# Joint column instructions in a 3x3 convolution: two row combinations in one tile, both output columns read by one instruction

## The chip, the cores and the metric

The kernel runs on one core of one Trainium2 chip. The core has a matrix engine (TensorE, PE in the profile; its weight loads are a row of their own, PEld), a vector engine (VectorE, DVE), a scalar engine (ScalarE, ACT), GpSimd (POOL) and SyncE (SP), each with its own queue of instructions; DMA queues are filled from SP, ACT and POOL. [...] The metric is the device time of one launch in microseconds, the median of the runs of the kernel. All data are float32.

## The reference

Two residual bottleneck blocks, one after the other, on 64 images of 1024 channels and 14x14 points. Each block is

```
out = relu(bn(conv1x1(x,   w1)  + b1))     # 1024 -> 256
out = relu(bn(conv3x3(out, w2)  + b2))     # 256 -> 256, padding 1
out = bn(conv1x1(out, w3) + b3)            # 256 -> 1024
out = relu(x + softplus(residual_scale) * out)
```

with `bn` the normalization by mean and variance over all images and points. The change lies in the 3x3 convolution (`conv2`), which runs once a block.

## The kernel before, in words

**The whole.** A first stage computes the 1x1 convolution of block 0 (0 to 307 us). Then, for each block, come `conv2`, the statistics of the third convolution, and the third convolution with the residual sum, which for block 0 is fused with the first convolution of block 1. `conv2` lies at about 307 to 602 us and 1292 to 1586 us. The activations of one block, `y_all`, stay in SBUF: 128 partitions, 2 channel slots, 8 groups (`NG`) of 8 images (`GI`). Within a group the rows come first: a row (`LINE`) is 8 images x 14 columns = 112 elements, and the columns of an image are stored as seven odd ones and then seven even ones, so a half row is one column of a pair.

**The arithmetic of `conv2` (L540).** It is a fast 3x3 convolution. Along the rows, a tile of four output rows is made from six row combinations of the input, one for each of `NF` = 6 transformed filters (`us`, made in the first stage and kept in DRAM). They are used in pairs: filters 1 and 2, 3 and 4, 5 and 0 (`order`, L542). Filters 3 and 4 need three tiles of rows (`full`), the others four (`RT`). Within a row combination `r`, every pair of columns is made from three inputs, by `Input.make` (L601): `sums` (the sum of both columns), `diffs` (their difference) and `v` (steps between neighbours of the same parity, whose two edge columns are copied by ACT, L612 and L613). `sums` and `diffs` have 448 elements a partition (336 for three tiles), `v` 768 (576), without its edges.

**The matmuls.** `Products` (L678) holds one filter of one group. Its four kinds of matmul are `m` (on `sums`), `l` (on `diffs`), `even` and `odd` (on `v`), each as two output slots times two input slots; the profile counts eight records for each. ACT copies `m` out of its bank into the banks `even` and `odd` (L710 with the bias, L712), PE adds the `v` products there, ACT copies `l` into SBUF as `ls` (L719), and DVE forms the output columns: even + ls and odd - ls (`add`, L744, recorded at L753). The banks are `l`, `m`, `odd` and `even`, two of each.

**The order of PE.** All matmuls are kept in program order (`matmul`, L167). The loop at L908 runs over 48 filters: `l` of this filter, `even`, then `m` of the next filter with ACT's copies, a long piece of ACT work (`long_work`, L888: the normalization of the next group, or moments of the group before), then `odd`. After that the outputs of this filter go to `finish` (L765), and one more filter's inputs are made, three filters ahead (L906 and L923). PE, in its own order, waits at an `m` until its `sums` are there, and at an `l` until its `diffs` are.

**DVE.** What it does in a group is: the row combinations (`combine`, L576: for filters 1 and 2 four scaled sums `t`, L646 and L647, and `ra`, `rb`; for 3 and 4 two differences and two scaled sums; for 5 and 0 two further differences, L668 and L673, and two scaled sums), six times `make`, six times the two output columns, and the sums that put the output rows together in `finish` (`fa`, `fb`, `fc`, and the four rows of `y`). In the first six groups (`by_transfer`, L772) the last filter's outputs go to `y` and the sum `a` of the earlier ones is added by two accumulating DMAs on POOL (L836). Except where `keep_in_program_order` is called, the order of DVE and ACT is planned when the kernel is built, from the order of the program and from what is ready; it is then fixed. Buffers are counted per name in `BUFS` (L70); a name that isn't in it has one.

## Time and profile before

Median of three runs: 1988.76 us (1988.5 to 1989.09).

| What | Profiled execution |
|---|---|
| span, first to last instruction | 1985.8 us |
| PE matmul | 1925.8 us, 97% |
| PE weight load | 1619.0 us, 82% |
| DVE | 1603.6 us, 81% |
| ACT | 976.0 us, 49% |
| POOL | 541.0 us, 27% |
| granted PE clock, mean | 0.990 |
| chain that ended last | PE 88%, DVE 6%, DMA 3%, ACT 1%, issue 1% |

The median lies 3.0 us above the span of the profiled execution. In the profile's lines the first fields are start and duration in us, the engine, the line of the kernel (helpers have one line for all their calls: every matmul is at L169, every scaled sum at L572), the operation, and output<-inputs by tile names. A number in square brackets is how long the engine had been idle, with what released it. Busy shares are means over stages with different limits, so a stage must be looked at by itself.

### The profile page before, as it was taken

The numbers are of one execution on the slowest core, as the hardware profiler recorded it, in microseconds if no ns is written. First come the engines' busy times: TensorE is split into PE (matmuls) and PEld (weight loads), VectorE is DVE, ScalarE is ACT, GpSimd is POOL, SyncE is SP. The second block draws the span as 40 slices with busy tenths as digits, with TensorE's granted clock in tenths as the row PEclk, the third lists the DMA queues.
The fourth block names the chain that finished last, engine by engine and source line by source line (L and its number), as shares of the span: only waits on it lengthen the run. The fifth ranks groups of instructions, "written<-read, shape, count | busy, mean of one in ns | idle before, by whom it ended". The sixth has DMA issues, their size and how long they took to land.

```text
span 1985.8 us, 27403 instructions
## 1 busy us (share of the span) xinstructions
PE 1925.8 (97%) x9432; PEld 1619.0 (82%) x9432; DVE 1603.6 (81%) x2890; ACT 976.0 (49%) x2007; POOL 541.0 (27%) x638
## 2 busy tenths in 40 slices
PE   8999998999998999999999999989999899999998
PEld 5555557999997889999999999989999887555554
DVE  5778758999998566776777777699999975899997
ACT  1222214566665055555555555446666641555555
POOL 0111100100105134334333433201010050666665
PEclk9999999999998999999999999999999999999999
DMA  7776724676747534444444444257666375699998
GB/s 288 272 257 240 255 98 155 183 206 185 204 143 201 194 130 163 177 182 162 181 177 163 184 173 163 98 181 204 198 186 206 122 196 207 247 335 337 340 340 296
DMA packets 188985, 408.41 MB, mean 206 GB/s; under 512 B 24944, under 2 KB 165136, under 8 KB 172336
## 3 DMA queue, kind: packets, MB, share of 16 engines
q1 hardware_dynamic: 161728, 324.66, 47.6%
q0 software_dynamic: 21504, 30.94, 6.7%
q10 hardware_dynamic: 5616, 51.06, 6.1%
q8 instruction: 75, 1.23, 0.2%
q14 instruction: 62, 0.51, 0.1%
HBM read 263.75 MB, written 115.34 MB: 191 GB/s over the span
## 4 chain that ended last, share of the span: by engine, by line
PE 88%; DVE 6%; DMA 3%; issue 1%; ACT 1%; SPq 0%; POOL 0%; DVEq 0%; ACTq 0%; POOLq 0%
PE ay L169 17%; PE cy L169 14%; PE cp L169 11%; PE ap L169 10%; PE even L169 7%; PE m L169 7%; PE odd L169 7%; PE l L169 7%; PE ax L169 5%; PE cx L169 4%; DVE x L447 2%; DMA x<-mid 1%; PE ps L169 1%; DVE x L505 1%; DMA out<-x 1%
## 5 line engine op out<-in xcount | busy, mean ns | idle before, releaser
L321 ACT ACTIVATE cu<-cy,scale 128x196 f32<-128x196 f32 (+1 forms) x552 | 257.0, 474 | 295.1 <-PE cy L169 287.4
L321 ACT ACTIVATE x<-x,shift 128x392 f32<-128x392 f32 x368 | 212.0, 614 | 69.8 <-POOL x L473 53.2
L447 DVE SCALAR_TENSOR_TENSOR x<-cp,scale,x 128x196 f32<-128x196 f32 (+1 forms) x368 | 177.9, 483 | 82.0 <-PE cp L169 81.0
L169 PE MATMUL cy<-ct,ws 128*128 128x196 f32 (+1 forms) x736 | 221.7, 383 | 2.5 <-ACT cu L321 2.5
L468 POOL TENSOR_TENSOR x<-x,cu 128x196 f32<-128x196 f32 (+1 forms) x184 | 167.7, 911 | 170.5 <-ACT cu L321 170.4
L169 PE MATMUL ay<-at,ws 128*128 128x196 f32 (+1 forms) x752 | 209.3, 381 | 1.0 <-ACT au L321 1.0
L473 POOL TENSOR_TENSOR x<-x,cu 128x392 f32<-128x392 f32 x124 | 126.1, 1017 | 190.8 <-DVE x L447 186.1
L169 PEld LDWEIGHTS ay<-at,ws 128*128 128x128 f32 x752 | 136.3, 190 | 35.1 <-ACT au L321 1.9
L169 PEld LDWEIGHTS cy<-ct,ws 128*128 128x128 f32 x736 | 133.5, 190 | 37.0 <-ACT cu L321 4.1
L169 PE MATMUL m<-sums,ua 128*128 128x224 f32 (+1 forms) x752 | 146.5, 338 | 15.9 <-issue 15.9
L169 PE MATMUL even<-v,ub 128*128 128x224 f32 (+1 forms) x768 | 151.3, 338 | 0.0
L169 PE MATMUL odd<-v,ub 128*128 128x224 f32 (+1 forms) x768 | 151.0, 337 | 0.0
L169 PE MATMUL l<-diffs,ub 128*128 128x224 f32 (+1 forms) x768 | 148.8, 336 | 0.0
L494 POOL TENSOR_TENSOR x<-x,cu 128x392 f32<-128x392 f32 x120 | 125.2, 1044 | 82.2 <-DVE x L447 73.3
L169 PEld LDWEIGHTS m<-sums,ua 128*128 128x128 f32 x752 | 130.5, 189 | 20.7 <-issue 20.4
L836 POOL DMA_DIRECT2D y<-fa x24 | 31.1, 1530 | 414.5 <-ACT ls L719 225.6
L169 PEld LDWEIGHTS even<-v,ub 128*128 128x128 f32 x768 | 135.4, 189 | 1.5
L169 PEld LDWEIGHTS odd<-v,ub 128*128 128x128 f32 x768 | 134.9, 188 | 1.3
L169 PEld LDWEIGHTS l<-diffs,ub 128*128 128x128 f32 x768 | 134.6, 189 | 0.5
L321 ACT ACTIVATE au<-ay 128x196 f32<-128x196 f32 (+1 forms) x141 | 53.6, 380 | 156.9 <-PE ay L169 156.3
L447 DVE SCALAR_TENSOR_TENSOR x<-cx,scale,x 128x196 f32<-128x196 f32 (+1 forms) x184 | 89.1, 484 | 49.9 <-PE cx L169 49.6
L169 PE MATMUL cy<-y,w 128*128 128x196 f32 (+1 forms) x404 | 126.4, 399 | 0.0
(216 smaller groups left out, 4256.7 us busy)
## 6 DMA issues: line engine op xcount, KB each, us to landing
x<-in_x SPq DMA_DIRECT2D x62, 1568.0 KB, 6.6
ub<-u SPq DMA_DIRECT2D x94, 768.0 KB, 4.9
x<-mid SPq DMA_DIRECT2D x32, 1568.0 KB, 9.9
mid<-x ACTq DMA_DIRECT2D x31, 1568.0 KB, 5.1
out<-x SPq DMA_DIRECT2D x123, 392.0 KB, 7.0
ua<-u SPq DMA_DIRECT2D x94, 256.0 KB, 3.0
u<-y POOLq DMA_DIRECT2D x48, 256.0 KB, 6.0
home<-y SPq DMA_DIRECT2D x90, 96.0 KB, 3.8
```

Source lines behind the costliest of these rows:

```text
L169: tc.keep_in_program_order(nc.tensor.matmul(*args, **kw))
L321: tc.keep_in_program_order(nc.scalar.activation(*args, **kw))
L447: nc.vector.scalar_tensor_tensor(v, bank, self.scale[:, o : o + 1], v, ALU.mult, ALU.add)
L468: nc.gpsimd.tensor_add(self.part(1, 1), self.part(1, 1), u3)
L473: nc.gpsimd.tensor_add(v, v, self.u12)
L494: nc.gpsimd.tensor_add(v, v, self.u12[:, i * self.n : (i + 1) * self.n])
L505: nc.vector.tensor_scalar(v, v, self.shift[:, o : o + 1], 0.0, ALU.add, ALU.max)
L836: nc.gpsimd.dma_start(out=out_rows[0][:, o], in_=a[:, o], accum_op=ALU.add)
```

## The change

The two filters of a pair get one tile each for `r`, `v`, `sums` and `diffs` (class `Inputs`), and `sums`, `v` and `diffs` are made by one instruction for both (`add_columns`, `step_columns`, `subtract_columns`). The sums of both are issued before the first filter of the pair is handed on, the steps and differences after it, that is one turn of the loop later; only the first pair of the first group still does it by filter and by slot. The four `t` become two (two neighbouring rows at once), the row differences of filters 3, 4, 5 and 0 are one instruction over twelve rows of both slots (tile `steps`), and filter 0's input takes its rows out of it by ACT copies. `even` and `odd` become one tile of two banks (`columns`), two buffers; ACT copies `l` twice, as +l and -l, and one DVE instruction forms both output columns. In the first six groups the first output row is now written from `a` and `c` (with its last line by an ACT copy), and the accumulating DMA adds the last filter's outputs, from `f`. Buffers: `v`, `sums` and `diffs` two (of pairs), `r`, `steps` and `fa` one, `f` three; before, `r` and `t` had four, `fa` two.

```diff
@@ -67,7 +67,7 @@
 GPX = GI * HW
 RT, NF = 4, 6
 LINE = GI * W
-BUFS = dict(ua=3, ub=3, t=4, r=4, sums=3, diffs=4, v=3, ls=3, f=2, fa=2)
+BUFS = dict(ua=3, ub=3, sums=2, diffs=2, v=2, ls=3, f=3)
 PARTS = 4
@@ -544,9 +543,14 @@
         each = list(itertools.product(range(MS), range(MS)))
-        for tag in COLUMNS * 2:
+        def columns():
+            return psum.pool.tile([P, 2, 512], FP, tag="columns", name="columns", bufs=2)
+        for banks in (columns(), columns()):
             n = MS * RT * GI * WH
-            matmul(psum.tile(n, tag), ident, ident[:, :1].to_broadcast([P, n]), start=True, stop=True)
+            for q in (ODD, EVEN):
+                matmul(banks[:, q, :n], ident, ident[:, :1].to_broadcast([P, n]), start=True, stop=True)
         full = RT - 1
@@ -566,59 +570,60 @@
         def last(to, g, k, by, s=slice(0, MS)):
...
+            nc.scalar.activation(to[:, s], y_grp[:, s, g, 4 * (RT - 1) + k - 1, :], AF.Copy, scale=by)
         def stt(to, a, by, c):
             return nc.vector.scalar_tensor_tensor(to, a, by, c, ALU.mult, ALU.add)
...
+        both = slice(0, MS)
+        steps = []
+        def scratch():
+            return pool.tile([P, MS * 4 * full * LINE], FP, tag="steps", name="steps")
+        class Inputs:
+            def __init__(self, pair, run):
+                self.pair, self.run = pair, run
+                self.tiles = tiles = full if pair[0] == 3 else RT
+                self.lines = lines = tiles * GI
+                n = len(pair) * MS * lines
+                def part(tag, width):
+                    v = pool.tile([P, 2 * MS * RT * GI * width], FP, tag=tag, name=tag, bufs=BUFS.get(tag, 1))
+                    return v[:, : n * width].rearrange("p (k s l c) -> p k s l c", k=2, s=MS, c=width)
+                self.r, self.v = part("r", W), part("v", W)
+                self.sums, self.diffs = part("sums", WH), part("diffs", WH)
+            def rows(self, k):
+                return self.r[:, k].rearrange("p s (r i) w -> p s r (i w)", i=GI)
+            def add_columns(self, k=slice(0, 2), s=both):
+                r = self.r[:, k, s]
+                self.run(nc.vector.tensor_add(self.sums[:, k, s], r[:, :, :, :, WH:], r[:, :, :, :, :WH]))
+            def step_columns(self, k=slice(0, 2), s=both):
+                r, v = self.r[:, k, s], self.v[:, k, s]
+                q = r.rearrange("p k s l (q c) -> p (k s l) q c", q=2)
+                self.run(
+                    nc.vector.tensor_sub(
+                        v[:, :, :, :, 1 : W - 1].rearrange("p k s l (q c) -> p (k s l) q c", q=2),
+                        q[:, :, :, 1:], q[:, :, :, : WH - 1],
                     )
...
+                )
+                nc.scalar.activation(v[:, :, :, :, 0], r[:, :, :, :, 0], AF.Copy)
+                nc.scalar.activation(v[:, :, :, :, W - 1], r[:, :, :, :, W - 1], AF.Copy, scale=-1.0)
+            def subtract_columns(self, k=slice(0, 2), s=both):
+                r = self.r[:, k, s]
+                self.run(nc.vector.tensor_sub(self.diffs[:, k, s], r[:, :, :, :, :WH], r[:, :, :, :, WH:]))
+            def products(self, g, k):
+                i = self.pair[k]
                 first = g == 0 and i == order[0][0]
                 u = {}
@@ -631,49 +636,72 @@
                             in_=us[b][i][:, part, :, a:e].rearrange("p s o k m -> p (s o) (k m)"),
                         )
                     u[a] = v
...
+                return Products(i, self.lines, self.v[:, k], self.sums[:, k], self.diffs[:, k], u, first)
+        def combine(g, pair, before=None):
+            def run(ins):
+                if before is not None:
+                    tc.keep_in_program_order(ins)
+            x = Inputs(pair, run)
+            ra, rb = (x.rows(k) for k in range(2))
             if pair[0] == 1:
...
+                t = scratch()[:, : MS * RT * 2 * LINE].rearrange("p (s r l) -> p s r l", s=MS, r=RT)
+                t2, t1 = t[:, :, :, :LINE], t[:, :, :, LINE:]
                 slots = [both] if before is None else [slice(s, s + 1) for s in reversed(range(MS))]
                 for part in slots:
                     if before is not None:
                         before(part.start)
...
+                    last(t1[:, :, RT - 1], g, 2, -3.0, part)
+                    last(t2[:, :, RT - 1], g, 1, -3.0, part)
                     for s in range(part.start, part.stop):
...
+                        two_rows = y_all[:, s, g * GPX : g * GPX + 4 * full * LINE]
+                        two_rows = two_rows.rearrange("p (r h l) -> p r h l", r=full, h=2)
+                        run(stt(t[:, s, :full], two_rows[:, :, 0], -4.0, two_rows[:, :, 1]))
                     run(nc.vector.tensor_add(ra[:, part], t1[:, part], t2[:, part]))
...
+                    if before is not None:
+                        for make in x.add_columns, x.step_columns, x.subtract_columns:
+                            make(slice(0, 1), part)
                 nc.vector.tensor_sub(rb, t1, t2)
...
+                if before is None:
+                    x.add_columns()
+                else:
+                    for make in x.add_columns, x.step_columns, x.subtract_columns:
+                        make(slice(1, 2))
             elif pair[0] == 3:
...
+                d = scratch().rearrange("p (s f) -> p s f", s=MS)
+                y = y_all[:, :, g * GPX : (g + 1) * GPX]
+                ins = nc.vector.tensor_sub(d, y[:, :, 2 * LINE :], y[:, :, : (H - 2) * LINE])
+                if g == 0:
+                    tc.keep_in_program_order(ins)
+                steps[:] = [d.rearrange("p s (r k l) -> p s r k l", k=4, l=LINE)]
+                d = steps[0]
+                stt(ra, d[:, :, :, 0], 2.0, d[:, :, :, 1])
+                stt(rb, d[:, :, :, 0], -2.0, d[:, :, :, 1])
+                x.add_columns()
             else:
...
+                d = steps[0]
+                last(ra[:, :, RT - 1], g, 1, -1.0)
+                r5, r0 = (r[:, :, :full] for r in (ra, rb))
+                stt(r5, d[:, :, :, 0], -4.0, d[:, :, :, 2])
+                nc.scalar.activation(rb[:, :, 0], y_grp[:, :, g, 1], AF.Copy, scale=-1.0)
+                nc.scalar.activation(rb[:, :, 1:full], d[:, :, : full - 1, 3], AF.Copy, scale=-1.0)
+                nc.scalar.activation(rb[:, :, RT - 1], d[:, :, full - 1, 3], AF.Copy, scale=-4.0)
+                stt(r0, r0, 4.0, d[:, :, :, 1])
+                x.add_columns()
+            yield x.products(g, 0)
+            if before is None:
+                x.step_columns()
+                x.subtract_columns()
+            yield x.products(g, 1)
         class Products:
@@ -701,10 +729,11 @@
             def start(self):
                 self.ls = None
-                self.banks = {q: self.bank(COLUMNS[q]) for q in (EVEN, ODD)}
+                self.banks = columns()[:, :, : MS * self.n].rearrange("p q (o n) -> p q o n", o=MS)
                 if not self.first:
                     m = self.whole("m", SUM, self.sums)
-                    for v in self.banks.values():
+                    for q in (EVEN, ODD):
+                        v = self.banks[:, q]
                         if self.i == 1:
                             for o in range(MS):
                                 nc.scalar.activation(v[:, o], m[:, o], AF.Identity, bias=par[:, B2 + o : B2 + o + 1])
@@ -714,9 +743,10 @@
             def middle(self):
                 l = self.whole("l", DIFF, self.diffs)
-                ls = pool.tile([P, MS * RT * GI * WH], FP, tag="ls", name="ls", bufs=BUFS["ls"])
-                self.ls = ls[:, : MS * self.n].rearrange("p (o n) -> p o n", o=MS)
-                nc.scalar.activation(self.ls, l, AF.Copy)
+                ls = pool.tile([P, 2 * MS * RT * GI * WH], FP, tag="ls", name="ls", bufs=BUFS["ls"])
+                self.ls = ls[:, : 2 * MS * self.n].rearrange("p (q o n) -> p q o n", q=2, o=MS)
+                for q, sign in (EVEN, 1.0), (ODD, -1.0):
+                    nc.scalar.activation(self.ls[:, q], l, AF.Copy, scale=sign)
             def columns(self, *qs):
                 parts = {ODD: [(D3M1, self.r[:, :, :, WH:])], EVEN: [(D0M2, self.r[:, :, :, :WH])]}
@@ -731,36 +761,33 @@
                 opened = set()
                 for q, o, (k, v), s in steps:
                     matmul(
...
+                        self.banks[:, q, o].rearrange("p (l c) -> p l c", c=WH), self.filter(s, o, k), v[:, s],
                         start=self.first and q not in opened, stop=True, skip_group_check=True,
                     )
                     opened.add(q)
...
+            def by_columns(self, v):
+                return v.rearrange("p q o (l c) -> p q (o l) c", c=WH)
+            def add_to(self, f):
+                to, v, ls = halves(f), self.by_columns(self.banks), self.by_columns(self.ls)
                 if self.first:
...
+                    for q, o in itertools.product((EVEN, ODD), range(MS)):
+                        one = [w[:, q].rearrange("p (o l) c -> p o l c", o=MS)[:, o] for w in (to, v, ls)]
                         bias = par[:, B2 + o : B2 + o + 1]
...
+                        nc.vector.scalar_tensor_tensor(one[0], one[1], bias, one[2], ALU.add, ALU.add)
                 else:
...
+                    nc.vector.tensor_add(to, v, ls)
+                return f
+        def halves(f):
+            return f.rearrange("p o r (i q c) -> p q (o r i) c", i=GI, q=2)
         def outputs(c):
...
+            return c.add_to(new("f", c.lines // GI))
         def finish():
@@ -792,7 +819,12 @@
                 for o in range(MS):
                     stt(out_rows[1][:, o, :full], e[:, o], 2.0, d3[:, o])
                     stt(out_rows[2][:, o], c[:, o], 4.0, a3[:, o])
-                nc.vector.tensor_add(a3, a3, c)
+                if by_transfer:
+                    nc.vector.tensor_add(out_rows[0][:, :, :full], a3, c)
+                    nc.scalar.activation(out_rows[0][:, :, full], a[:, :, full], AF.Copy)
+                else:
+                    nc.vector.tensor_add(a3, a3, c)
                 stt(d3, e, 8.0, d3)
                 if g == 0:
                     begin(out_rows[1][:, :, :full])
@@ -813,27 +845,20 @@
                     merge()
                 cb = yield
...
+                if by_transfer:
+                    f = outputs(cb)
+                    for o in range(MS):
+                        nc.gpsimd.dma_start(out=out_rows[0][:, o], in_=f[:, o], accum_op=ALU.add)
+                    continue
+                nc.vector.tensor_add(halves(a), halves(a), cb.by_columns(cb.ls))
+                for j, q in enumerate((EVEN, ODD)):
                     for o in range(MS):
                         to, more = (
                             v[:, o].rearrange("p r (i q c) -> p q r i c", i=GI, q=2)[:, q] for v in (out_rows[0], a)
                         )
...
+                        nc.vector.tensor_add(to, cb.banks[:, q, o].rearrange("p (r i c) -> p r i c", r=RT, c=WH), more)
                     stat(2 + j, [out_rows[0][:, o].rearrange("p r (i q c) -> p q r i c", i=GI, q=2)[:, q] for o in range(MS)])
...
             yield
         def entry(eng, half, count, mean, var):
@@ -1293,7 +1318,7 @@
         stats2 = keep.tile([P, MS, 1 + PARTS, nc.vector.BN_STATS_DIM], FP, tag="stats2", name=f"stats2_{b}")
         with tc.tile_pool(name=f"conv2_{b}", bufs=1) as pool, ExitStack() as scope:
-            conv2(Psum(scope, ["l"], l=2, m=2, odd=2, even=2), pool, b, pb, aff, affine_of, stats2)
+            conv2(Psum(scope, ["l"], l=2, m=2), pool, b, pb, aff, affine_of, stats2)
         with tc.tile_pool(name=f"last_{b}", bufs=1) as one, tc.tile_pool(
             name=f"last_x_{b}", bufs=4 if b == 0 else 5
```

(Where many lines are taken out, "..." stands for them: they are the lines of the kernel before that are shown above.)

## The prediction

> **What bounds the kernel now.** I read the page's busy table first, then its groups, then stretches of one group of images inside the two 3x3 stages (307 to 602 us and 1292 to 1586 us, by the tiles of the convolution), last the order of time. The groups of the page: the four kinds of matmul of this stage.
>
> ```profile
> L169 PE MATMUL m<-sums,ua 128*128 128x224 f32 (+1 forms) x752 | 146.5, 338 | 15.9 <-issue 15.9
> L169 PE MATMUL even<-v,ub 128*128 128x224 f32 (+1 forms) x768 | 151.3, 338 | 0.0
> L169 PE MATMUL l<-diffs,ub 128*128 128x224 f32 (+1 forms) x768 | 148.8, 336 | 0.0
> ```
>
> Of the four kinds (odd is like even) only m waits: 15.9 us in both layers. The stretches (us, then busy time and count of PE, PEld, DVE, ACT, POOL) show a rhythm of 34.82 us a group:
>
> ```profile
> 350.00:385.00 35.00, 33.44 (x192) 32.91 (x191) 34.91 (x59) 21.02 (x45) 2.65 (x2) 1.00 0.69 190
> 385.00:420.00 35.00, 33.94 (x195) 33.40 (x194) 34.92 (x59) 22.49 (x47) 2.55 (x2) 1.00 0.69 195
> ```
>
> DVE has no gap at all (34.92 of 35), PE is short of full by one gap a group, ACT has 12 us free. The gap, in order of time:
>
> ```profile
> 384.05 0.62 DVE L753 TENSOR_TENSOR f<-even,ls 128x448 f32<-128x448 f32 x1
> 384.08 1.69 PE L169 MATMUL even<-v,ub 128*128 128x224 f32 x8
> 384.59 1.08 DVE L648 TENSOR_TENSOR r<-t 128x896 f32<-128x896 f32 x1
> 385.59 0.62 DVE L753 TENSOR_TENSOR f<-odd,ls 128x448 f32<-128x448 f32 x1
> 386.12 0.61 DVE L603 TENSOR_TENSOR sums<-r 128x448 f32<-128x448 f32 x1
> 386.83 1.75 PE L169 MATMUL m<-sums,ua 128*128 128x224 f32 x8 [1.06 <-issue]
> ```
>
> PE is done with even at about 385.8; the first m of the next group needs sums, which DVE ends at 386.7. The page calls the releaser "issue", but m starts 0.1 us after sums ends. So the stage is bound by DVE, with PE 1.06 us a group behind it: 34.82 - 1.06 = 33.76 us is PE's own need. There are seven such gaps a layer, the first longer (1.55 at 350.5), 15.9 in 14, mean 1.14. That is the ceiling of what any relief of DVE brings here; the 1x1 stages are not touched.
>
> **What DVE saves.** Durations overlap, so I take start to start: 448 elements 0.53 (385.59 to 386.12), 896 elements 1.00 (384.59 to 385.59). One instruction of twice the size saves 2 x 0.53 - 1.00 = about 0.065 us; an element costs 1.04 ns. Instructions of a group, before and after: filters 1, 2: four t, two r, six sums/v/diffs become two, two, three (-5). Filters 3, 4: two t, two r, six become one, two, three (-4). Filters 5, 0: four, six become two, three (-5; two of the row differences now lie in the one large one). Outputs: five times two and four become six (-8). The closing row sums keep their number. Elements stay equal. 59 - 22 = 37 instructions; 22 x 0.065 = 1.43 us; DVE needs 34.8 - 1.4 = 33.4 us a group, just below PE's 33.76.
>
> Forms that the trace does not show: steps of 2688 elements, v of 1536, one read over two banks of PSUM. The nearest rows are the same operations at half size: v of 768 takes 951 ns, which is what 0.618 us for 448 plus 320 x 1.04 ns gives, so its stride of 6 costs nothing; f from PSUM takes 616 ns, sums from SBUF 617. I take 1.43. [...] The lower end is a two-bank read that costs as much as two (6 x 0.065 less: 1.04 us); below that I have no reason for a loss.
>
> **What ACT gets.** A second copy of l a filter (448 elements start to start 0.45, 336 0.34): +2.5 us a group. Edge columns of v in 6 instead of 12 instructions (0.20 each now, about 0.27 at double size): -0.8. Filter 0's rows by three copies where there was a scaling and DVE's difference: +0.5; the last row of y: +0.3. Together +2.5 on 22.5, 25 of 33.8 us: hidden under the idle 12. l ends two matmul runs (3 us) ahead of the sum that reads it, so the extra 0.45 is covered; uncovered it would be 6 x 0.45 = 2.7 us a group. DMA: the same weight loads on SP, the same two accumulating transfers a group on POOL, now out of f (three buffers) and not fa; nothing waits for them until the moments of the next group.
>
> **What the change makes later.** Number a group's filters 0 to 5 in order of use. Sums of the first of a pair now need both combinations (+1.0 us, and half of the joint sum, +0.47). Steps and differences are issued one filter later, behind that filter's output. And r and steps have one buffer: the next pair's first write waits for the DVE work on the last pair and for ACT's edge copies. Worked in the order of the program, from the end of filter 3's odd matmuls: f 0.77, c and e 1.53, four row sums 1.66, two more 1.53, t 1.53, r and r 2.0, joint sums 1.0: 10.0 us. PE reaches the next m after six runs of 1.52 = 9.12. Then f 1.0, rows 1.07, v 1.67, diffs 1.0: 14.7, where PE reaches the next l after eight runs, 12.16. With 0.2 us of hand-over at each end, the gap would be 15.1 - 12.2 = 2.9 us a group in place of 1.14, unless 2.9 us of t, r and r (4.5 us in all) run ahead of f. Behind a waiting l stand even, the next m and odd on PE, and ACT's copies behind those.
>
> Does DVE have that time? From filter 0's output to filter 3's, PE takes 15.3 us; DVE then has 3.0 + 5.5 + 3.4 = 12.0 us of work: 3.3 spare, just enough. Will the order use it? DVE's order is fixed when the kernel is built, but not in the order of the program; the trace shows work brought forward:
>
> ```profile
> 399.05 0.85 DVE L668 TENSOR_TENSOR r<-y 128x672 f32<-128x672 f32 x1
> 401.33 0.62 DVE L753 TENSOR_TENSOR f<-even,ls 128x448 f32<-128x448 f32 x1
> ```
>
> The row difference of filter 4 stands behind that output in the program and runs 2.3 us before it, and that even was ready on PE at about 399.3: the planner's pace of PE is near the real one. So I expect it to fill most of the spare time.
>
> [...] Now DVE is saturated (34.92 of 35) and fewer instructions win; but at 33.4 of 33.8 after it no longer is. By the row the gap goes (-15.9 us)[...]. [...]
>
> **The sum.** 15.9 - 14 x 0.2 = 13.1 us. Head of each layer: two t fewer before the first sums, 2 x 0.08 a layer, 0.3 in both; the large steps instruction (2.9 us for 1.6) is covered there, since sums of filter 2 end 4.6 us before their m at 328.9. Tail: one joint sum, under 0.1. Span 1985.8 - 13.4 = 1972.4; the median of the runs lies 3.0 above that span, so 1975.4, I say **1975.5 us**, 0.67% faster.
>
> **Rivals.** (a) Only part is brought forward: half a microsecond of gap is left a group: 15.9 - 7 = 8.9, about 1980; up to 0.85 left, 1984.8. For it: lumps of 1.7 and 2.9 us fill badly. (b) Slower: steps and differences come too late at l, the 2.9 us gap: 14 x 2.9 - 15.9 = +25, 2013. It decides from the point where less than 1.8 us is brought forward (2.9 - 1.14). For it: one r buffer and the later issue; against it: 3.3 us spare and the row at 399.05. (c) Nothing moves: the gain on DVE is taken back by waits for PE's odd at the joint reads, 1988.8 within 4 us. (d) The saving isn't there, because the fixed cost is hidden latency: also 1988.8; the pair 0.53 and 1.00 speaks against it. (e) ACT becomes late: needs 9 us more than counted; very small.
>
> **From these to numbers.** Likeliest, with at most 0.45 us a gap left (1972.5 to 1979): 0.62. (a) 0.15, (c) and (d) 0.10, (b) with its smaller forms 0.13. The runs differ by 0.6 us; 0.2% is 4 us, about what a measurement tells from no change. Faster 0.77, same 0.10, slower 0.13. Range: the ceiling 15.9 + 0.4 gives 1972.5, 1 us below for an uncertain base, and up to 1987 to hold (a) and half of (c).
>
> **What would show it.** DVE's count in 35 us falls from 59 to about 37 and gaps appear on it; m's idle falls below 4 us with no new one at l; a group repeats every 33.8 to 34.0 us. Wrong: idle in front of l with diffs as releaser (b), DVE waiting for odd (c), a v of 1536 elements or a joint f well over 1.7 or 1.1 us (d).

## The result, and the profile after

The changed kernel takes **1982.39 us** (median of four runs, 1981.61 to 1983.14); the kernel before, on the same chip in the same session, 1988.92 (1988.5 to 1989.69). The ratio is 0.9965, 95% interval 0.9951 to 0.998: 6.5 us faster, where 13.4 were forecast. The profiled execution has a span of 1980.2 us, before 1985.8.

The page of the kernel after, its groups (busy us, mean ns, then the idle time ahead and what ended it); even and odd are now one tile, `columns`. Filters are called by the names of the code here; in the order of use they are 1, 2, 3, 4, 5, 0.

```profile
L168 PE MATMUL columns<-v,ub 128*128 128x224 f32 (+1 forms) x1536 | 302.1, 338 | 0.7 <-ACT columns L741 0.7
L168 PE MATMUL l<-diffs,ub 128*128 128x224 f32 (+1 forms) x768 | 149.6, 338 | 5.6 <-issue 3.2
L168 PE MATMUL m<-sums,ua 128*128 128x224 f32 (+1 forms) x752 | 145.9, 337 | 3.1 <-DVE sums L607 3.1
```

The 15.9 us in front of m have become 3.1 in front of m, 5.6 in front of l and 0.7 in front of columns: 9.4 in place of 15.9. The same two stretches as before (busy time and count of PE, PEld, DVE, ACT, POOL):

```profile
350.00:385.00 35.00, 32.44 (x185) 31.94 (x186) 34.21 (x37) 22.68 (x45) 2.65 (x2) 1.00 0.65 182
385.00:420.00 35.00, 35.00 (x202) 34.75 (x201) 34.35 (x39) 26.06 (x51) 2.54 (x2) 1.00 0.70 204
```

The second has what was forecast: 39 instructions on DVE, not 59, gaps on it, PE full. But DVE is still 34.35 of 35 us busy, and the first stretch, with the boundary of groups 0 and 1, is worse than before (PE 32.44, before 33.44).

A group can be clocked exactly by the first matmul of filter 3's m, the first m with 168 elements. From its start to that of the next group, in us:

| | first boundary | the six after it, layer 1 | sum of the six |
|---|---|---|---|
| before | 35.32 | 34.82 each (one 34.83) | 208.93 |
| after, layer 1 | 36.72 | 33.51, 33.91, 34.08, 34.12, 34.04, 34.72 | 204.38 |
| after, layer 2 | 36.72 | | 204.76 |

The account of one stage, from the first `ident` matmul to the first `cy` of the next stage (layer 1 / layer 2): up to the first such m 22.07 / 21.90 before, 21.92 / 21.99 after; first boundary +1.40 / +1.39; the six groups -4.55 / -4.17; the end of the stage 29.55 / 29.54 before, 28.95 both after. That is -3.90 and -3.28, together -7.2. Everything else took 1.6 us more in this one execution, so the span fell by 5.6; the medians, by 6.5, lie between.

**Two places** hold what is missing. The first boundary, in order of time, DVE and then PE (`steps` holds the two scaled sums t of the next group):

```profile
339.86 1.62 DVE L576 SCALAR_TENSOR_TENSOR steps<-y 128x672 f32<-128x672 f32 x2
341.40 0.85 DVE L782 TENSOR_TENSOR f<-columns,ls 128x672 f32<-128x672 f32 x1
342.17 1.08 DVE L665 TENSOR_TENSOR r<-steps 128x896 f32<-128x896 f32 x1
...
343.94 1.08 DVE L669 TENSOR_TENSOR r<-steps 128x896 f32<-128x896 f32 x1
...
347.38 0.85 DVE L824 TENSOR_TENSOR y<-fa,fc 128x672 f32<-128x672 f32 x1
...
348.92 0.91 DVE L875 BATCH_NORM_STATS2 first_stats<-y 128x6 f32<-128x336 f32 x2
349.75 0.16 DVE L877 BATCH_NORM_AGGREGATE mv_first<-first_stats 128x2 f32<-128x6 f32 x1
349.83 1.06 DVE L607 TENSOR_TENSOR sums<-r 128x896 f32<-128x896 f32 x1
...
351.94 1.75 DVE L613 TENSOR_TENSOR v<-r 128x1536 f32<-128x1536 f32 x1
...
354.68 1.08 DVE L623 TENSOR_TENSOR diffs<-r 128x896 f32<-128x896 f32 x1
```

```profile
350.94 1.78 PE L168 MATMUL m<-sums,ua 128*128 128x224 f32 x8 [1.08 <-DVE sums L607]
352.56 1.69 PE L168 MATMUL columns<-v,ub 128*128 128x224 f32 x8
355.87 1.75 PE L168 MATMUL l<-diffs,ub 128*128 128x224 f32 x8 [1.61 <-issue]
```

t runs ahead of filter 4's output f, and both r run ahead of the row sums. But `sums` stands behind all the row sums of group 0 and its first moments, as in the program, and ends at 350.9; `diffs` stands behind `v` and the closing rows and ends at 355.8. PE waits 1.08 and then 1.61: 2.69 us. One group later the planned order is another:

```profile
379.60 1.08 DVE L607 TENSOR_TENSOR sums<-r 128x896 f32<-128x896 f32 x1
380.60 0.85 DVE L816 TENSOR_TENSOR fc<-f 128x672 f32<-128x672 f32 x1
381.36 1.75 DVE L613 TENSOR_TENSOR v<-r 128x1536 f32<-128x1536 f32 x1
...
385.48 0.85 DVE L824 TENSOR_TENSOR y<-fa,fc 128x672 f32<-128x672 f32 x1
...
388.01 1.08 DVE L623 TENSOR_TENSOR diffs<-r 128x896 f32<-128x896 f32 x1
```

Now `sums` and `v` run ahead of the row sums, and PE waits for neither: the work was brought forward as forecast, but from the second boundary on. In the first group DVE is also later against PE. The joint `sums` of filters 5 and 0, first of group 0, then of group 1:

```profile
335.42 1.09 DVE L607 TENSOR_TENSOR sums<-r 128x896 f32<-128x896 f32 x1
```

```profile
367.65 1.09 DVE L607 TENSOR_TENSOR sums<-r 128x896 f32<-128x896 f32 x1
```

They start 7.1 us after filter 3's m (328.35) in group 0, and 2.6 us after it (365.07) in group 1.

The other place is filters 5 and 0 of every group, DVE and then ACT:

```profile
398.65 0.85 DVE L623 TENSOR_TENSOR diffs<-r 128x672 f32<-128x672 f32 x1
399.60 0.86 DVE L576 SCALAR_TENSOR_TENSOR r<-steps 128x672 f32<-128x672 f32 x1
400.76 0.86 DVE L576 SCALAR_TENSOR_TENSOR r<-r,steps 128x672 f32<-128x672 f32 x1 [0.30 <-ACT r L696]
401.73 1.09 DVE L607 TENSOR_TENSOR sums<-r 128x896 f32<-128x896 f32 x1
```

```profile
399.59 0.39 ACT L573 ACTIVATE r<-y 128x224 f32<-128x224 f32 x1 [1.32 <-DVE diffs L623]
399.89 0.37 ACT L695 ACTIVATE r<-y 128x224 f32<-128x224 f32 x1
400.17 0.56 ACT L696 ACTIVATE r<-steps 128x448 f32<-128x448 f32 x1
```

Other instructions of 672 elements take 0.77 start to start (380.60 to 381.36, 0.76). Here it is 0.95, 1.16 and 0.97: 0.77 us over, in every group. `r` has one buffer, so neither DVE nor ACT may write the r of filters 5 and 0 before the joint `diffs` of filters 3 and 4 has read the old one; then filter 0's scaled sum waits for ACT's copies (L695, L696), which stand behind another copy, L573.

### The profile page after: what moved, and what is told of

The parts are those of the page before. It is cut to its first block, busy times and chain, and to the rows that moved or that the text cites. A ratio compares the mean times of both kernels' runs of the same rounds, so it can differ in the third digit from the quotient of the medians.

```text
span 1980.2 us, 27057 instructions
## 1 busy us (share of the span) xinstructions
PE 1926.9 (97%) x9432; PEld 1619.1 (82%) x9432; DVE 1582.8 (80%) x2554; ACT 1017.1 (51%) x2039; POOL 540.6 (27%) x638
## 4 chain that ended last, share of the span: by engine, by line
PE 84%; DVE 10%; DMA 3%; issue 1%; ACT 1%; POOL 0%; DVEq 0%; SPq 0%; ACTq 0%
PE ay L168 17%; PE cy L168 14%; PE columns L168 11%; PE cp L168 11%; PE ap L168 10%; PE m L168 5%; PE l L168 5%; PE ax L168 5%; PE cx L168 4%; DMA x<-mid 2%; DVE x L446 2%; DMA out<-x 1%; PE ps L168 1%; DVE x L504 1%; DVE f L782 1%
## 5 line engine op out<-in xcount | busy, mean ns | idle before, releaser
L168 PE MATMUL columns<-v,ub 128*128 128x224 f32 (+1 forms) x1536 | 302.1, 338 | 0.7 <-ACT columns L741 0.7
L168 PEld LDWEIGHTS columns<-v,ub 128*128 128x128 f32 x1536 | 270.4, 189 | 4.4 <-ACT columns L741 1.2
L852 POOL DMA_DIRECT2D y<-f x24 | 31.1, 1533 | 411.7 <-DVE f L782 411.7
L168 PE MATMUL cx<-y,w 128*128 128x196 f32 (+1 forms) x404 | 125.3, 396 | 0.0
L168 PE MATMUL cp<-zt 128*128 128x257 f32 x392 | 120.1, 388 | 1.7 <-DVE zt L1010 1.7
```

The lines of the kernel that those rows point to most:

```text
L168: tc.keep_in_program_order(nc.tensor.matmul(*args, **kw))
L852: nc.gpsimd.dma_start(out=out_rows[0][:, o], in_=f[:, o], accum_op=ALU.add)
```

## The experiments

There were two theories for the half that did not come. **Theory 1**: DVE still bounds the groups, since some of its saving is lost in new waits on it. **Theory 2**: steps and differences come one filter too late, and PE waits for the chain to l, whatever DVE's total. Lines are told by the clock of the groups as above, because the whole runs of one changed kernel lie 1.5 us (the changed kernel) to 7.3 us (e7) apart, in part by the granted clock (last section).

**e1, less work on DVE.** The closing rows of a group, 672 and 224 elements, are left out, 1.07 us of DVE; the fourth row of each tile keeps what was there.

```diff
-                nc.vector.tensor_add(out_rows[3], d3, fa[:, :, :full])
-                nc.vector.tensor_add(end, d[:, :, full], fa[:, :, full])
```

> The changed kernel without the two closing row sums of y (out_rows[3] and end, 1.07 us of DVE a group from start to start); the fourth row of each tile keeps its old values. In DVE's order these stand behind diffs, so nothing that PE waits for at l is ahead of less work within one group. Theory 1 (DVE is still the bound: a group takes its 34.08 us because DVE has that much, 0.8 of it new waits at filters 5 and 0): a group falls to PE's own 33.5 to 33.6, the waits at l go, 6 to 8 us faster than the changed kernel, about 1975. Theory 2 (steps and differences are issued a filter too late, a chain from the outputs of one filter to l): the wait at l stays 0.3 us a group, within 2 us of 1982.4.

1971.93 us (1969.63 to 1973.88), ratio 0.9916 (0.9901 to 0.9931): 10.5 under the changed kernel, more than expected. Its stretch from 385 to 420 us, and its PE at the first boundary:

```profile
385.00:420.00 35.00, 35.00 (x202) 34.77 (x201) 34.35 (x38) 25.73 (x51) 2.55 (x2) 1.00 0.72 208
```

```profile
351.62 1.78 PE L168 MATMUL m<-sums,ua 128*128 128x224 f32 x8 [1.08 <-DVE sums L607]
...
355.48 1.75 PE L168 MATMUL l<-diffs,ub 128*128 128x224 f32 x8 [0.55 <-PE columns L168]
```

After the first boundary PE has no wait left in layer 1, and the six groups take 33.51, 33.51, 33.52, 33.51, 33.52, 33.51. So theory 1 holds for the groups, and **PE's own need is 33.51 us a group**, not the 33.76 of the prediction: a stop costs PE more than the idle time that the row shows (last section). Before, 1.06 of idle made 34.82 - 33.51 = 1.31 longer, and in e7 below 0.97 made 1.21: 0.24 to 0.25 on top. At the first boundary the wait at l falls by 1.06, what was taken from DVE: there the closing rows stand directly ahead of `diffs`.

**e2 and e3, a tile of its own for the r of filters 3 and 4.** It fits only with `ua` and `ls` at two buffers; e2 is that alone.

```diff
-BUFS = dict(ua=3, ub=3, sums=2, diffs=2, v=2, ls=3, f=3)
+BUFS = dict(ua=2, ub=3, sums=2, diffs=2, v=2, ls=2, f=3)
...
-                self.r, self.v = part("r", W), part("v", W)
+                if pair[0] == 3:
+                    r = pool.tile([P, n * W], FP, tag="r34", name="r34", bufs=1)
+                    self.r = r.rearrange("p (k s l c) -> p k s l c", k=2, s=MS, c=W)
+                else:
+                    self.r = part("r", W)
+                self.v = part("v", W)
```

> The control for the next one: the changed kernel with two buffers in place of three for ua and ls, to make room in SBUF. Both theories: within 1.5 us of 1982.4, since ls is read three matmul runs before its buffer is wanted again and the weights land in 3 us; if it is slower, the loads were closer to the edge than that.

> As the control, with a tile of its own for the row combinations of filters 3 and 4, so that those of 5 and 0 need not wait until diffs of 3 and 4 has read the one buffer. Theory 1: DVE's 0.18 before and 0.3 to 0.6 us within the row combinations of 5 and 0 go, a group falls to 33.6, 4 to 6 us faster than the control, about 1977. Theory 2: no change at l, within 1.5 us of the control.

e2: 1982.19 (1980.9 to 1982.46), as the changed kernel. e3: 1980.14 (1978.57 to 1981.79), ratio 0.9958 (0.9943 to 0.9973): 2 us, not separable from e2 by these runs; by the clock, its seven boundaries are 0.8 to 0.9 us a layer shorter than in e2. The waits ahead of the scaled sums are gone, but the planned order changed with it, and PE now waits elsewhere, 4.0 us in front of columns:

```profile
492.81 1.80 PE L168 MATMUL columns<-v,ub 128*128 128x224 f32 x8 [1.26 <-ACT columns L744]
```

**e4, ACT's row copies first.**

```diff
-                last(ra[:, :, RT - 1], g, 1, -1.0)
                 r5, r0 = (r[:, :, :full] for r in (ra, rb))
-                stt(r5, d[:, :, :, 0], -4.0, d[:, :, :, 2])
                 nc.scalar.activation(rb[:, :, 0], y_grp[:, :, g, 1], AF.Copy, scale=-1.0)
                 nc.scalar.activation(rb[:, :, 1:full], d[:, :, : full - 1, 3], AF.Copy, scale=-1.0)
+                last(ra[:, :, RT - 1], g, 1, -1.0)
+                stt(r5, d[:, :, :, 0], -4.0, d[:, :, :, 2])
```

> The changed kernel, only the order of ACT's copies for filters 5 and 0 changed: the two that filter 0's scaled sum waits for are issued first, the last row of filter 5 after them. Theory 1: DVE's wait for ACT (0.30 us a group shown, 0.39 from start to start) goes, a group is 0.3 us shorter, 3 to 4 us faster, about 1979. Theory 2: within 1.5 us of 1982.4.

1977.8 us (1976.57 to 1978.95), ratio 0.9945 (0.9928 to 0.9961). DVE at filters 5 and 0:

```profile
397.64 0.85 DVE L623 TENSOR_TENSOR diffs<-r 128x672 f32<-128x672 f32 x1
398.59 0.86 DVE L576 SCALAR_TENSOR_TENSOR r<-steps 128x672 f32<-128x672 f32 x1
399.47 0.86 DVE L576 SCALAR_TENSOR_TENSOR r<-r,steps 128x672 f32<-128x672 f32 x1
400.43 1.09 DVE L607 TENSOR_TENSOR sums<-r 128x896 f32<-128x896 f32 x1
```

1.16 has become 0.88; the other two, where an instruction needs the end of the one just ahead of it, stay. The six groups sum to 202.86 and 202.88, 1.5 and 1.9 less than in the changed kernel: 3.4 us in both layers, of the 4.6 between the medians; the end of the stage takes 0.36 more in each (29.31). The wait for ACT was one of the causes. The first boundary is unchanged (1.07 and 1.61).

**e5, the first moments later.** `begin`, about 1.1 us of DVE at the end of group 0, is moved behind the last outputs of that group.

```diff
                 stt(d3, e, 8.0, d3)
-                if g == 0:
-                    begin(out_rows[1][:, :, :full])
...
                     f = outputs(cb)
+                    if g == 0:
+                        begin(out_rows[1][:, :, :full])
```

> The changed kernel with the mean estimate of the first group (begin: two statistics, two aggregates, one scaling, 1.2 us of DVE) moved from ahead of the second group's first sums to behind the first group's last outputs. The first boundary alone waits 1.08 us at m and 1.61 at l in each layer, 5.4 us in both. Theory A (the statistics stand in the chain that leads to sums and diffs of the second group): m's wait goes and l's falls below 0.6 us, 3 to 4 us faster than the changed kernel, about 1979. Theory B (the chain is late there because r, steps and differences come late, whatever stands between): within 1.5 us of 1982.4.

1981.81 us (1978.96 to 1982.52): nothing. Its PE at the first and the second boundary:

```profile
349.69 1.78 PE L168 MATMUL m<-sums,ua 128*128 128x224 f32 x8 [0.18 <-DVE sums L607]
...
354.47 1.75 PE L168 MATMUL l<-diffs,ub 128*128 128x224 f32 x8 [1.48 <-issue]
```

```profile
385.35 1.78 PE L168 MATMUL m<-sums,ua 128*128 128x224 f32 x8 [0.16 <-DVE sums L607]
...
390.13 1.75 PE L168 MATMUL l<-diffs,ub 128*128 128x224 f32 x8 [1.48 <-issue]
```

The first boundary takes 35.68 in place of 36.72, the second 35.66 in place of 33.51. So the moments are not the cause: the first boundary gives 1.0 back, and the second, where they now stand, loses 2.2.

**e6, steps and differences of filters 1 and 2 one filter earlier.**

```diff
                 if before is None:
                     x.add_columns()
+                    x.step_columns()
+                    x.subtract_columns()
...
-            if before is None:
+            if before is None and pair[0] != 1:
                 x.step_columns()
                 x.subtract_columns()
```

> The changed kernel with the steps and differences of filters 1 and 2 issued before the first of them is handed on, as the kernel before did, and not one filter later. The number and size of instructions stay. Theory 1 (DVE is the bound): l's waits of 0.3 us a group go, but others come in their place, a group stays at 34.0 us; only the first boundary may gain, within 2 us of 1982.4. Theory 2 (issued too late): about 5 us faster, 1977.

1987.47 us (1985.54 to 1989.54): 5 us slower than the changed kernel, which neither theory had. No l waits any more, but every group has this:

```profile
392.28 1.80 PE L168 MATMUL columns<-v,ub 128*128 128x224 f32 x8 [0.50 <-ACT columns L741]
```

(0.95 to 0.97 in the later groups), 13.0 us in all, and a group takes 34.74. With steps and differences (2.7 us) ahead of it, DVE reads an output late, its bank comes free late, ACT's copies of m wait for the bank (3.7 us of idle for DVE's f before the one at 390.44), and PE for the copies. Theory 2 falls as a way to gain: the lateness moves from l to columns when the order is changed and DVE's total is not.

**e7, the joint read undone.**

```diff
-                    nc.vector.tensor_add(to, v, ls)
+                    for q in (EVEN, ODD):
+                        nc.vector.tensor_add(to[:, q], v[:, q], ls[:, q])
```

> The changed kernel with the joint read of both output columns undone: two DVE instructions, one for each column, from the same two-bank tile. Six more DVE instructions a group. If the fixed cost of an instruction is what is saved (0.067 us from start to start), a group takes 0.4 us longer, 12 x 0.4 = 5 us slower than the changed kernel, about 1987. If the joint read has cost something of its own (waiting for the odd column, a read over two banks), this one is the same or faster.

**e11, the joint read alone,** in the kernel before: `columns` and the two copies of l as in the change, everything else as before (`ls` two, `diffs` three buffers, to fit).

```diff
-            for q in c.banks:
-                c.add(q, half(f, q), c.column(q))
+                    nc.vector.tensor_add(to, v, ls)
...
-                nc.scalar.activation(self.ls, l, AF.Copy)
+                for q, sign in (EVEN, 1.0), (ODD, -1.0):
+                    nc.scalar.activation(self.ls[:, q], l, AF.Copy, scale=sign)
```

> The kernel before with only the joint read: even and odd in one tile of two banks, l copied twice, one DVE instruction for both output columns of filters 1, 2, 3, 4 and 5 (five fewer on DVE in each of the first six groups); row combinations, sums, steps and differences by filter as before; ls has two buffers and diffs three, to fit. By the prediction's price, 5 x 0.065 = 0.33 us a group on a stage that DVE bounds: 14 x 0.33 = 4.6, about 1983.7. By what separate reads cost in e7 (0.64 us a group for six, 0.107 each): 0.53 a group, 7.5 us, about 1981: then the joint inputs bring nothing. If a joint read waits for odd where the even half could have started earlier, DVE stands idle in the stage and the time is 1987 to 1990.

e7: 1989.23 us (1984.92 to 1992.19), ratio 1.0005 (0.9996 to 1.0013); a group takes 34.72. e11: 1981.54 us (1980.8 to 1982.53), ratio 0.9969 (0.9957 to 0.998). With joint inputs and no joint read there is no gain, with the joint read and no joint inputs there is all of it, as far as these runs can tell. In e11 DVE remains saturated, and m waits 9.2 us in place of 15.9; its stretch and its group:

```profile
385.00:420.00 35.00, 33.67 (x193) 33.12 (x192) 34.97 (x55) 25.42 (x56) 2.54 (x2) 1.00 0.67 194
```

```profile
L169 PE MATMUL m<-sums,ua 128*128 128x224 f32 (+1 forms) x752 | 146.5, 338 | 9.2 <-DVE sums L608 9.2
```

The six groups of layer 1 take 205.76, 0.53 less each than before: more than five times 0.065, because some short waits of DVE go as well. It also has an even start: its first boundary is 34.82 and its second 35.12, with none of the 36.72 of the joint inputs.

**e8, closing rows on GpSimd** in the first six groups, with the edits of e4 and e5.

```diff
-                nc.vector.tensor_add(out_rows[3], d3, fa[:, :, :full])
-                nc.vector.tensor_add(end, d[:, :, full], fa[:, :, full])
+                eng = nc.gpsimd if by_transfer else nc.vector
+                eng.tensor_add(out_rows[3], d3, fa[:, :, :full])
+                eng.tensor_add(end, d[:, :, full], fa[:, :, full])
```

> A candidate: the changed kernel with ACT's two copies for filter 0 first, the mean estimate of the first group late, and the closing row sums of the first six groups on POOL, which is idle in this stage but for two transfers a group. Theory 1: DVE has 1.4 us a group less, PE waits at neither m nor l but in the first group, as in the run without those sums: about 1970 to 1973. If POOL and DVE get in each other's way in SBUF, DVE's other instructions grow longer and it stays above 1976.

1984.6 us (1981.84 to 1986.01), ratio 0.9979 (0.9971 to 0.9987): worse than e4, and not the 1970 to 1973 of the first theory. The first boundary is nearly healed (0.19 at m, 0.41 at l), but columns waits for ACT 8.5 us in all, most of it in the later groups (2.52 at 460.3), where the planned order is another. DVE's instructions also took longer beside GpSimd's, as the expectation had allowed for. The addition of group 1 on GpSimd and DVE's next two scaled sums, then the same two in e4:

```profile
385.86 6.93 POOL L838 TENSOR_TENSOR y<-fb,f 128x672 f32<-128x672 f32 x1 [26.86 <-DVE f L781]
```

```profile
392.23 2.51 DVE L576 SCALAR_TENSOR_TENSOR r<-steps 128x672 f32<-128x672 f32 x2
```

```profile
392.94 1.62 DVE L576 SCALAR_TENSOR_TENSOR r<-steps 128x672 f32<-128x672 f32 x2
```

GpSimd's addition ends at 392.79, 0.56 us after the first of the two scaled sums has begun, and the two take 2.51 us together, in e4 1.62: 0.89 us more, most of the 1.07 us taken from DVE. What the two engines share there was not shown.

**e9 and e10, the repairs together.** e9 is e4 with e5's edit, e10 is e4 with e3's.

> The changed kernel with ACT's two row copies for filter 0 issued before the scaled sum of filter 5 (as in e4, 1977.8 us), and the first moments moved behind the last outputs of group 0 (as in e5, which gained nothing alone). If the first group boundary is late because of what DVE has in a row and not because of the moments, this is within 1.5 us of e4: 1976.5 to 1979.5. If the moments were the cause there, and e5 only could not show it because every group lost time anyway, the 3.2 us of idle in front of l and the 2.1 us in front of m in e4 go down by half: about 1975.

> The changed kernel with both repairs of filters 5 and 0: a tile of their own for the row combinations of filters 3 and 4 (with ua and ls at two buffers, as in e3, 1980.1 us) and ACT's row copies first (as in e4, 1977.8 us). If the two remove different waits of DVE, it is below both: the group at 33.5 us or PE's own need, 1975.5 to 1977. If each removes the same wait, 1977 to 1979. If the free order again pulls work ahead into stretches in which PE then waits at columns for ACT, as in e3, it is above e4: 1979 to 1981, with more than 3 us of idle in front of the columns matmuls.

e9: 1976.94 us (1975.79 to 1981.42), e10: 1980.27 (1976.47 to 1980.57). e9 has e5's pattern (l waits 1.48 and 1.43 at the first two boundaries) and is not separable from e4. In e10 three groups run at PE's own pace (33.51, 33.52, 33.60), and then two take 35.50 and 34.26, with 1.27 and 0.48 in front of columns: the same as e3, and the third case of its expectation.

**e12, a lead for DVE in the first two groups:** e9, and the closing rows of groups 0 and 1 alone on GpSimd.

```diff
+                eng = nc.gpsimd if g < 2 else nc.vector
+                eng.tensor_add(out_rows[3], d3, fa[:, :, :full])
+                eng.tensor_add(end, d[:, :, full], fa[:, :, full])
```

> ACT's row copies first (e4, 1977.8 us; with the later first moments, e9, 1976.9), and DVE relieved in the first two groups alone: the first moments behind the last outputs of group 0, the closing rows of groups 0 and 1 (1.07 us of DVE each) on GpSimd. Theory: at the first group boundary DVE is merely a fixed amount behind PE, because the joint inputs need a larger lead of DVE and the lead has to be made once, in the first groups; each microsecond taken from DVE there takes one from the first boundaries, about 1.07 x 2 a layer, so 4 us in all: 1972.5 to 1975. In e8, with the same in all of the first six groups, the first boundary had fallen to 0.19 in front of m and 0.41 in front of l. Rival: the order that is planned changes with it and PE waits elsewhere (as in the third group of e8, 2.5 us in front of columns): 1977 to 1980.

1976.63 us (1974.14 to 1977.15), ratio 0.9937 (0.9923 to 0.9951), between the two expectations. The first boundary falls from 36.70 to 34.62 in layer 1, as the theory had it, but the three groups after it take 34.14, 33.62 and 34.45 in place of e4's 33.52, 33.51 and 34.26: 0.9 of the 2.1 is given back. It is the fastest of the full kernels by its median, faster than both kernels of this document; from e4 and e9 it can't be told apart.

## Why the prediction was right and wrong

The sign was right, and so was the bound, DVE; the size was twice what came. The time lies inside the range, but where rival (a) had been put, above the likeliest stretch. By its steps, for one layer:

| Step | Forecast | Measured, layer 1 / 2 |
|---|---|---|
| head | -0.15 | -0.15 / +0.09 |
| first boundary | -1.36 (gap 1.56 to 0.2) | +1.40 / +1.39 |
| six later boundaries | -5.2 (1.06 to 0.2 each) | -4.55 / -4.17 |
| end of the stage | under -0.1 | -0.60 / -0.59 |

**The step that failed is the 0.2 us a group of "The sum", left for work that is not brought forward and taken for all 14 gaps alike.** It was the author's estimate; no row stands behind it. The condition, that work must run ahead, had been worked out right; it was then tested only on rows from the middle of the stage. At the first boundary DVE is 4.5 us later against PE than one group on. Of the chain only t runs ahead of f there; `sums`, `v` and `diffs` stand behind the row sums, as in the program, and the first moments, 0.9 us that the working did not have, come on top. PE waits 2.69 us, by the mechanism of rival (b), once a layer; that this is so near the 2.9 of the working, which has t behind f and no moments, is luck. (The 4.5 us of "t, r and r" hold the joint sums too; by its own figures the three alone are 3.5. The 0.2 us of hand-over was an estimate; in the rows of the first boundary above, m starts 0.05 us after the end of `sums` and l 0.11 after that of `diffs`.) It behaves like a lead that DVE must have over PE and has to make once: e1 and e12 shorten the first boundary by 1.07 and 2.08, about what they take from DVE. That the joint inputs need the larger lead fits e11, which has none of this loss, and the prediction's +1.0 and +0.47; why the plan takes another order at the first boundary was not tested. Against the forecast this term is 2.75 us a layer, 5.5 of the 6.2 by which stage and forecast differ (13.4 less 7.2).

**That the six later boundaries came near the forecast is in part luck**: 0.76 and 0.70 us a group, where 0.86 was forecast. Two terms were wrong and hid each other, the saving on DVE and PE's need. With the whole saving of 1.43 a group would have come down to PE's 33.51, 1.31 shorter by these figures.

**What DVE saves: the price was right, the saving of 1.43 us was not.** Start to start, less 1.04 ns an element, every instruction that waits for nothing is 0.065 to 0.075 over, before and after, and 59 to 37 is what the counts show (37 to 39 in 35 us). But between 425 and 560 us the waiting ones together take 1.07 us a group more than that, before 0.32: 0.75 us of new waits. The three places at filters 5 and 0 that are shown above alone make 0.77. So 22 x 0.067 - 0.75 = 0.72, and the groups show 34.82 - 34.08 = 0.74. The prediction had looked at the one buffer of r only for what it makes late at m and l, not for what DVE and ACT themselves wait for at the next pair. e4 shows it for one of these waits; 0.20 of the 0.77 comes from no buffer, since the joint `sums` reads what the scaled sum just ahead of it writes. The joint read earned all of the net gain (e7, e11): the 14 instructions that the joint inputs remove are worth 0.9 us a group, and their waits and the first boundary take that back. This holds for the kernel as it was built: the seven boundaries of a layer sum to 241.1 and 241.5 us in it and to 240.6 in e11, but to 239.6 in e4, where joint inputs and joint read stand together and one wait is gone.

**PE's need was 0.25 us too high** (33.51, e1), so the ceiling of 15.9 us was too low: 14 gaps of 1.31, two of them longer, are some 19. e1, at 1971.93 below the 1972.5 of the forecast's ceiling, fits that.

**The forms** were right: joint f of 896 elements from two banks 1.00 start to start (355.68 to 356.68), v of 1536 1.67 (381.36 to 383.03), and an e11 in which f from `columns` has the same 0.067 over as sums from SBUF. So a read from PSUM cost no more here than one from SBUF: `fa` of 896 elements, from SBUF, takes 1.00 start to start as well.

**ACT** got what was counted, 25.1 to 26.1 us in 35, before 22.5. "Hidden under the idle 12" was wrong in one place: the copies of filter 0's rows stand right on DVE's path (e4).

**What the larger instructions make late** can be weighed with e11, in which the inputs are not joined: its first boundary is 1.9 us shorter than the changed kernel's (34.82 for 36.72), and its later groups are on average 0.2 longer. Of the +25 us of rival (b), what came is the first boundary.

**Rivals.** (a), a part of the gap left, came nearest: 9.4 us of idle in place of 15.9, more of it at l (5.6) than at m (3.1). Idle at l was also the sign named for (b). (c) is absent: the joint reads wait 2.8 us in both layers together (0.9 at 896 elements, 1.9 at 672), and the separate ones had waited 3.7. (d) is ruled out by the rows of 896. Of (e), only the wait at L696 and 0.7 us in front of columns.

## What to carry to other kernels

Fewer instructions on the engine that bounds are worth their fixed price (0.067 us each here) only as long as they bring no wait on that engine: whoever joins tiles and takes their buffers to one should follow the next writer of each tile, on every engine, and not only its readers. When work must run ahead, look at the start of the loop, where little is ahead yet, as a case of its own. And try the parts singly: here the small part, one read in place of two, was the whole gain of the kernel as built.

## What the runs showed of the hardware

A stop of PE at m or l cost 0.24 to 0.28 us more than its idle time in the row (1.06 made a group 1.31 longer, 0.97 made it 1.21 longer, and 1.33 in e11 made it 1.61 longer). The rows of PE show where it comes from, in the kernel before (`even` and m are in the lines of the prediction, 384.08 and 386.83):

```profile
388.42 1.69 PE L169 MATMUL odd<-v,ub 128*128 128x224 f32 x8
```

A run of eight matmuls has a row of 1.67 to 1.69 us, but the next run normally starts 1.51 to 1.53 us after it, so that the rows overlap by 0.16; idle time is counted from the end of the row and leaves this out. And the run after the stop takes 1.59 us to the start of the next (386.83 to 388.42), 0.08 more. That makes 1.06 + 0.16 + 0.08 = 1.30.

An addition of 672 elements took 3.8 us on GpSimd in e8 on average (2.2 to 6.9), on DVE 0.85. Its group in layer 1, 307 to 602 us:

```profile
L838 POOL TENSOR_TENSOR y<-fb,f 128x672 f32<-128x672 f32 x6 | 22.7, 3791 | 176.2 <-DVE f L781 137.1 <-DMA ub<-u 39.0
```

At the head of layer 1, after waits of 1.3 and 3.2 us, the granted PE clock was not the same in every execution. The stretch from 318 to 324 us, first of the changed kernel, then of e4, with the same matmuls (the clock is the first number after the counts of POOL):

```profile
318.00:324.00 6.00, 6.00 (x25) 5.65 (x24) 4.98 (x5) 0.00 (x1) 0.00 (x0) 0.72 0.16 47
```

```profile
318.00:324.00 6.00, 5.59 (x29) 5.56 (x30) 6.00 (x9) 1.25 (x4) 0.00 (x0) 1.00 0.23 74
```

The changed kernel takes 21.92 us to filter 3's m, e4 20.25. The kernel before and e12 have a mean of 0.72 in this stretch too. In the changed kernel the clock is 0.50 from 318.11 to 321.53 us and 1.00 before and after.

In the traces of the kernels before and after, the clock changes only on a grid of 3.41 us (in the changed kernel at 318.11 and 321.53, before at 318.51 and 321.92), and where this grid lies differs between the two. From 20 to 1970 us, full clock was halved six times in each. Four of the six follow an interval of the grid in which PE's rows fill 0 to 37% of the time: in the changed kernel the one from 314.70 to 318.11, with most of the wait of 3.2 us and PE busy for 0.65 us of 3.41, so such an interval need not be idle throughout. The other two follow an interval full of rows of matmuls with one output column (679.92 to 683.34 and 1659.55 to 1662.96 in the changed kernel). After every other interval at full clock, all with 43% or more, it stayed full. That e4 kept it after the same wait fits a grid that divides the wait between two intervals: 3.15 us in equal halves would leave PE busy in 54% of each, an estimate from these figures; where the grid lay in e4 is not shown.

So one execution takes 1.7 us more at the head of a layer, and another does not: after the wait of 3.15 to 3.16 us in layer 1 the first eight matmuls take 1.78 us in e2, e4, e5 and e7, and 2.01 to 2.75 in e1, e9, e12 and the changed kernel. It is a reason why executions of one kernel lie apart: of the five of e9, three with a mean clock of 0.992 took 1975.79 to 1976.94 us, two with 0.990 took 1980.1 and 1981.42. The profiled execution of e7, 0.993, is with 1984.92 the fastest of its twelve; the others have 0.990 or 0.991. The groups are free of it in both kernels: the clock is full from 321.53 to 598.00 and from 1301.15 to 1577.63 us in the changed kernel, before from 321.92 to 598.40 and from 1304.96 to 1584.85.
